# One 128-column product per 128 edges, with edge rows copied beside gathered rows, in a graph-attention kernel

## The chip, the cores and the metric

The kernel runs on one core of a Trainium2 chip. The metric is the device time of one execution in microseconds, the median of several runs. The core's engines are named as in the profile: PE (matrix products, with PEld for its weight loads), DVE (vector), ACT (scalar activation), POOL (here it issues the indirect gathers) and SP (here it issues plain transfers).

## The reference

A graph of 12500 nodes has 400000 edges, sorted by destination; every node and every edge has 64 features. One attention layer is computed, followed by a layer norm:

```
h_src = x[src];  h_dst = x[dst]
e     = leaky_relu(concat(h_src, h_dst, edge) @ W_attn + b_attn, 0.01)
m     = concat(h_src, edge) @ W_ne
alpha = softmax of e over the edges of one destination
z     = segment_sum(alpha * m, dst)
out   = relu(concat(x, z) @ W_out)
y     = layernorm(x + out)
```

## The kernel before

**Tiling.** Because sums over edges are linear, the kernel sums the weighted raw rows (edge row and gathered source row, 64 features each) per destination and applies `W_ne` once at the end. The sorted edges are cut into 782 groups of 512 (128 partitions, T = 4 edges on each). SG = 4 groups are a *part*, the unit of loads, scores and sums. Up to BG = 32 groups are a *batch*, the unit of the softmax; the list `sizes` holds 30, then 23 batches of 32, then 12 and 4.

**One batch** (the loop at the end of `sorted_path`) does the following.

- `gather` (L134) loads a part's edge rows into `ze` by one transfer of 512 KB on SP's queue, and issues one indirect gather on POOL for every 128 edges (L149), 16 for a part, into `zx`. The gathered row holds the 64 features of the source node and, from the second batch on, its share of the score as a 65th value. In the first batch the rows come from `x` itself, and the share is computed on DVE (L169 and L171).
- `scores` (L155) makes the score of each edge: DVE multiplies and reduces `ze` (L165, L167), adds the source's share (L172), builds the one-hot tile `hot` of each edge's slot among 48 consecutive destinations (L174), and picks the destination's share with it (L179, L182) out of `win`, which PE broadcasts from a row `wrow` (L161). L184 leaves the scores in `y`.
- `softmax` (L224) turns a batch's scores around (L252, then `e` on ACT, L254), runs scans on DVE with small products on PE between them, carries maximum and sum over to the next batch, and leaves `alpha` in PSUM (L309).
- `aggregate` (L321) makes `w` = `hot` times `alpha` on DVE (L324), multiplies on PE (L332), and adds the result to the running sums `acc` at the group's first destination on DVE (L342). Each float32 product is two PE instructions. For 128 edges there are two products, one of the edge rows, which goes to partitions 0 to 63 of `pg`, and one of the gathered rows, which goes to partitions 64 to 127. That is 64 PE instructions for a part.

**What sets the order.** A scheduler lays the operations out on the engines by their dependences and by the buffers of the pools; each engine then works in the order laid out. The pool `feats` holds ZB = 11 buffers each of `ze` and `zx`, so a gather waits until the `aggregate` eleven parts earlier has read its buffer. `hot` has HB = 9 buffers, `w` and `pg` have two each, `win` and `alpha` one each. A small PSUM tile `fixed` holds the slot numbers and two rows of attention weights. `indices` (L99) makes the gathers' indices `srcs` two batches ahead out of `raw` (transfer), `nat` (ACT, L112) and transposes on PE (L115). `neighbours` (L203) loads the destinations `d3` that the softmax's scans use, and fills the tile first when a batch has fewer than 32 groups.

**Start and end.** Before the batches, a prologue writes `table` (features and source shares) and `sdflat` (destination shares), spreads the latter with a transfer to `shifted`, and gathers from it 7 times on POOL (`wk`, L422) into `wins`, from which the rows `wrow` are read. Five parts' gathers are issued ahead of those 7 in the source (the list `ahead`). In the third batch and the ones after it, `own_part` (L432) is called after a part's `aggregate`, 25 times in all: it makes the product of `x` with its half of `W_out` and stores it in `early`. After the last batch, `finish_sorted` (L491) applies the weights to `acc` (L538), adds `early`, and makes the layer norm.

Of the kernel before, what the change touches and what calls it, by code (L numbers as in the profile page):

```python
# [9 lines left out]
F32 = mybir.dt.float32  # L10
I32 = mybir.dt.int32
AF = mybir.ActivationFunctionType
OP = mybir.AluOpType
AX = mybir.AxisListType

P = 128
T = 4
# [8 lines left out]
S = 48  # L26
BG = 32
SG = 4
HQ = 4
EW = 65  # L30
ZB = 11
HB = 9
NBC = 4

BF16 = mybir.dt.bfloat16
# [3 lines left out]
def sorted_path(ctx, tc, x, dst, idx, edge, w_ne, w_attn, b_attn, w_out, out, flag):  # L39
# [6 lines left out]
    nc = tc.nc  # L46
    N, D = x.shape
    E = edge.shape[0]
    NB = (N + P - 1) // P
# [33 lines left out]
    shifted = dram.tile([NB * P, S], F32, name="shifted")  # L83
# [7 lines left out]
    feats = loop.enter_context(tc.tile_pool(name="feats", bufs=ZB))  # L91
    psum = loop.enter_context(tc.tile_pool(name="psum", bufs=2, space=bass.MemoryType.PSUM))

    fixed = psum.tile([P, S + 2 * D], F32, name="fixed", bufs=1)
    slots = fixed[:, 0:S]
    w_edge = fixed[:, S:S + D].unsqueeze(1)
    w_src = fixed[:, S + D:S + 2 * D].unsqueeze(1)

    def indices(g0, G):  # L99

# [32 lines left out]

    def gather(g0, n, srcs, b0, plain):  # L134

        ze = feats.tile([P, SG, T, D], F32, name="ze")
        zx = feats.tile([P, SG, T, EW], F32, name="zx")
        whole = min(n, NG - 1 - g0)
        if whole:
            nc.sync.dma_start(out=ze[:, 0:whole].rearrange("p g t f -> p g (t f)"),  # L140
                              in_=edge[g0 * GE:(g0 + whole) * GE, :].rearrange("(g p t) f -> p g (t f)", g=whole, t=T))
        if whole < n:
            nc.vector.memset(ze[:, n - 1], 0.0)
            nc.sync.dma_start(out=ze[0:RP, n - 1],
                              in_=edge[E - REST:E, :].rearrange("(p t) f -> p t f", t=T))
        for g in range(n):
            for t in range(T):
                at = srcs[:, t, g0 + g - b0:g0 + g - b0 + 1]
                nc.gpsimd.indirect_dma_start(  # L149
                    out=zx[:, g, t, 0:D] if plain else zx[:, g, t, :], out_offset=None,  # L150
                    in_=x[:, :] if plain else table[:, :],
                    in_offset=bass.IndirectOffsetOnAxis(ap=at, axis=0))
        return ze, zx

    def scores(g0, n, ze, zx, drel, b0, y, plain):  # L155

        b = g0 - b0
        wrow = tiny.tile([1, SG, S], F32, name="wrow")
        nc.sync.dma_start(out=wrow[:, 0:n, :], in_=wins[g0:g0 + n, :].unsqueeze(0))
        win = psum.tile([P, SG, S], F32, name="win", bufs=1)  # L160
        nc.tensor.matmul(win[:, 0:n, :], ones_row, wrow[:, 0:n, :], start=True, stop=True)  # L161

        yb = y[:, :, b:b + n].rearrange("p t g -> p g t")
        prod = work.tile([P, SG, T, D], F32, name="prod", bufs=1)
        nc.vector.tensor_tensor(prod[:, 0:n], ze[:, 0:n],  # L165
                                w_edge.unsqueeze(1).to_broadcast([P, n, T, D]), op=OP.mult)
        nc.vector.tensor_reduce(yb, prod[:, 0:n], axis=AX.X, op=OP.add)  # L167
        if plain:
            nc.vector.tensor_tensor(prod[:, 0:n], zx[:, 0:n, :, 0:D],  # L169
                                    w_src.unsqueeze(1).to_broadcast([P, n, T, D]), op=OP.mult)  # L170
            nc.vector.tensor_reduce(zx[:, 0:n, :, D], prod[:, 0:n], axis=AX.X, op=OP.add)  # L171
        nc.vector.tensor_tensor(yb, yb, zx[:, 0:n, :, D], op=OP.add)  # L172
        hot = work.tile([P, SG, T, S], BF16, name="hot", bufs=HB)
        nc.vector.tensor_tensor(  # L174
            hot[:, 0:n], slots.unsqueeze(1).unsqueeze(1).to_broadcast([P, n, T, S]),
            drel[:, :, b:b + n].rearrange("p t g -> p g t").unsqueeze(3).to_broadcast([P, n, T, S]),
            op=OP.is_equal)
        at = work.tile([P, SG, T, D], F32, name="prod", bufs=1)[:, :, :, 0:S]
        nc.vector.tensor_tensor(at[:, 0:n], hot[:, 0:n],  # L179
                                win[:, 0:n].unsqueeze(2).to_broadcast([P, n, T, S]), op=OP.mult)  # L180
        sdst = tiny.tile([P, SG, T], F32, name="sdst")
        nc.vector.tensor_reduce(sdst[:, 0:n], at[:, 0:n], axis=AX.X, op=OP.add)  # L182
        nc.vector.tensor_tensor(sdst[:, 0:n], sdst[:, 0:n], yb, op=OP.add)
        nc.vector.scalar_tensor_tensor(yb, sdst[:, 0:n], SLOPE, sdst[:, 0:n], op0=OP.mult, op1=OP.max)  # L184
        return hot
# [38 lines left out]
    def softmax(G, y, d3, carry, first):  # L224


        R = HQ * G
# [77 lines left out]
                                sm.rearrange("r (q t) -> r q t", t=T), op=OP.mult)  # L305
        alpha0 = rows.tile([P, T, BG], F32, name="alpha0")
        nc.vector.transpose(alpha0.rearrange("p t g -> p (t g)"), al.rearrange("r t q -> r (t q)"))
        alpha = psum.tile([P, T, BG], F32, name="alpha", bufs=1)
        nc.scalar.activation(alpha, alpha0, AF.Copy)  # L309
        fac = None  # L310
        if not first:
# [4 lines left out]
            nc.tensor.matmul(pfac[:, 0:1], ones_row, fac1, start=True, stop=True)  # L316
            fac = tiny.tile([P, 1], F32, name="fac")
            nc.vector.tensor_copy(fac, pfac[:, 0:1])
        return alpha, fac, (top[:, R:R + 1], den[:, R:R + 1])

    def aggregate(g0, n, ze, zx, hot, alpha, b0, fac):  # L321
        b = g0 - b0
        w = work.tile([P, SG, T, S], F32, name="w")
        nc.vector.tensor_tensor(  # L324
            w[:, 0:n], hot[:, 0:n],
            alpha[:, :, b:b + n].rearrange("p t g -> p g t").unsqueeze(3).to_broadcast([P, n, T, S]),
            op=OP.mult)
        pg = psum.tile([P, SG, P], F32, name="pg")[:, :, 0:S]
        for g in range(n):
            for t in range(T):  # L330
                for at, z in ((0, ze), (D, zx)):
                    nc.tensor.matmul(pg[at:at + D, g, :], z[:, g, t, 0:D], w[:, g, t, :],  # L332
                                     start=(t == 0), stop=(t == T - 1))
        _, vs = nc.values_load_multi_w_load_instructions(
            d0i[0:1, g0:g0 + n], engines=(EngineType.DVE,), min_val=0, max_val=N - 1,
            skip_runtime_bounds_check_because=within)
        for g in range(n):
            if g == 0 and fac is not None:
                a1 = acc[:, ds(vs[0], 1)]
                nc.vector.tensor_scalar(a1, a1, fac, None, op0=OP.mult)  # L340
            ag = acc[:, ds(vs[g], S)]
            nc.vector.tensor_tensor(ag, ag, pg[:, g, :], op=OP.add)  # L342


    sizes = []
    left = NG
    for short in (SG, 3 * SG):
        sizes.insert(0, short)
        left -= short
    while left > 0:  # L350
        sizes.insert(0, min(left, BG))
        left -= sizes[0]
    starts = [sum(sizes[:k]) for k in range(len(sizes))]

# [22 lines left out]
    with tc.tile_pool(name="pre", bufs=2) as pre:  # L377
# [34 lines left out]
        zero = pre.tile([1, S], F32, name="zero", bufs=1)  # L412
        nc.vector.memset(zero, 0.0)
        nc.scalar.dma_start(out=sdflat[NB * P:NB * P + S].unsqueeze(0), in_=zero)
        while len(ahead) < 5 and (len(ahead) + 1) * SG <= sizes[0]:
            ahead.append(gather(len(ahead) * SG, SG, prepared[0][0], 0, True))
        over = sdflat[0:1]
        nc.sync.dma_start(out=shifted, in_=bass.AP(over.tensor, over.offset, [[1, NB * P], [1, S]]))
        for k in range(NW):
            m = min(P, NG - k * P)  # L420
            wk = pre.tile([P, S], F32, name="wk")
# [10 lines left out]
    def own_part(c0):  # L432
# [8 lines left out]
            nc.scalar.dma_start(out=xb[:, 0:nf, :],  # L441
                                in_=x[c0 * P:(c0 + nf) * P, :].rearrange("(b p) f -> p b f", p=P))
        xtt = work.tile([D, NBC, P], F32, name="xtt", bufs=1)
        pxt = psum.tile([P, NBC, P], F32, name="pg")
        for j in range(n):
            nc.tensor.transpose(pxt[0:D, j, :], xb[:, j, :], ident)
        nc.scalar.activation(xtt[:, 0:n, :], pxt[0:D, 0:n, :], AF.Copy)  # L447
        po = psum.tile([P, NBC, P], F32, name="pg")[:, :, 0:D]
        for j in range(n):
            nc.tensor.matmul(po[:, j, :], xtt[:, j, :], wout[:, 0, :], start=True, stop=True)  # L450
        xo = work.tile([P, NBC, D], F32, name="xo", bufs=1)
# [8 lines left out]
    with loop:  # L460
        carry = None
        own = 0
        ready = {k: prepare(k) for k in range(2)}
        for k, G in enumerate(sizes):
            b0 = starts[k]
            srcs, drel = ready.pop(k)
            d3 = neighbours(b0, G)
            y = rows.tile([P, T, BG], F32, name="y", bufs=2)
            if G < BG:
                nc.vector.memset(y[:, :, G:BG], 0.0)  # L470
            parts = []
            for g0 in range(b0, b0 + G, SG):
                n = min(SG, b0 + G - g0)
                ze, zx = ahead.pop(0) if ahead else gather(g0, n, srcs, b0, k == 0)
                hot = scores(g0, n, ze, zx, drel, b0, y, k == 0)
                parts.append((g0, n, ze, zx, hot))
            if k + 2 < len(sizes):
                ready[k + 2] = prepare(k + 2)
            alpha, fac, carry = softmax(G, y, d3, carry, k == 0)
            for g0, n, ze, zx, hot in parts:  # L480
                aggregate(g0, n, ze, zx, hot, alpha, b0, fac if g0 == b0 else None)
                if own < NB and k > 1:
                    own_part(own)
                    own += NBC
        while own < NB:
            own_part(own)
            own += NBC
# [518 lines left out]
```

## Time and profile before

| | us |
|---|---|
| median of 3 runs (lowest, highest) | 4106.01 (4105.14, 4106.99) |
| the profiled execution | 5109.14 |
| its span | 5107.4 |
| POOL busy in it | 2964.9 |
| DVE busy | 1708.1 |
| PE busy | 1410.6 |
| ACT busy | 109.6 |

The profiled execution is longer than the timed runs. Its mean granted PE clock is 0.547 of full speed. A row of the costliest groups reads: line, engine, operation, output and inputs with their shapes, number of instructions, then busy time and mean nanoseconds of one, then the idle time just before these instructions and what ended most of it. In a timeline a line gives the start, the duration, the instruction, and in brackets the idle time before it with its releaser; "issue" is time in which the engine waited for nothing that the profile shows.

### The profile page before, as it was taken

What the parts mean: (1) busy time and instruction counts of PE and PEld (TensorE: products, weight loads), DVE (VectorE), ACT (ScalarE), POOL (GpSimd) and SP (SyncE); (2) the same over time, 40 slices, a digit from 0 to 9 for tenths busy, and PEclk for the clock granted to TensorE, in tenths of its full rate; (3) what the DMA queues carried; (4) which work ended last, traced back from release to release, by engine and by line L of the source; (5) the groups of instructions that cost most, each with busy time, mean ns of one, the idle gap of its engine ahead of it and who ended that gap; (6) DMA issues with size and microseconds to landing.
All of it is one profiled execution on the core that took longest, in us unless ns stands there. A gap on an engine that the chain in (4) does not pass through costs nothing.

```text
span 5107.4 us, 39846 instructions
## 1 busy us (share of the span) xinstructions
PE 1410.6 (28%) x14238; PEld 1105.0 (22%) x14238; DVE 1708.1 (33%) x4006; ACT 109.6 (2%) x239; POOL 2964.9 (58%) x3142
## 2 busy tenths in 40 slices
PE   0022233443222222222222222222222222222226
PEld 0012122332222122212121212122222211221225
DVE  3333233232342332332323323323233233233346
ACT  0000000000000000000000000000000000000001
POOL 6645656556556556565565565655655655656550
PEclk9975555555555555555555555555555555555555
DMA  6111122222111112111111111111111211212113
GB/s 145 25 34 42 44 48 54 53 53 60 41 45 44 43 38 48 42 46 41 43 44 43 42 44 43 43 42 44 47 41 40 47 42 38 47 37 48 41 36 77
DMA packets 315273, 239.73 MB, mean 47 GB/s; under 512 B 160576, under 2 KB 264235, under 8 KB 315064
## 3 DMA queue, kind: packets, MB, share of 16 engines
q0 software_dynamic: 100320, 104.41, 10.6%
q1 hardware_dynamic: 147464, 116.22, 8.0%
q10 hardware_dynamic: 67280, 16.45, 1.6%
q8 instruction: 115, 1.88, 0.2%
q14 instruction: 94, 0.77, 0.1%
HBM read 226.98 MB, written 12.28 MB: 47 GB/s over the span
## 4 chain that ended last, share of the span: by engine, by line
issue 28%; POOL 26%; another core or an unknown queue 19%; DVE 14%; PE 10%; DMA 3%; DVEq 1%; ACT 0%; POOLq 0%; ACTq 0%
POOL zx L149 26%; PE pg L332 7%; DMA zx<-table,srcs 2%; DVE y L167 2%; DVE prod L165 2%; DVE sdst L182 1%; DVE prod L179 1%; PE sm L198 1%; PE sm L190 1%; DVE hot L174 1%; DVE w L324 1%; DVE by_row L195 0%; DVE b L271 0%; DVE acc L342 0%
## 5 line engine op out<-in xcount | busy, mean ns | idle before, releaser
L149 POOL DMA_INDIRECT zx<-table,srcs x3008 | 2840.6, 944 | 1951.4 <-issue 841.3
L332 PE MATMUL pg<-w,ze 128*64 128x48 f32 x6256 | 792.3, 297 | 1640.2 <-issue 985.1
L332 PEld LDWEIGHTS pg<-w,ze 128*64 128x64 f32 x6256 | 703.6, 213 | 1729.3 <-issue 1581.7
L332 PE MATMUL pg<-w,zx 128*64 128x48 f32 x6256 | 803.4, 297 | 613.2 <-issue 582.1
L324 DVE TENSOR_TENSOR w<-hot,alpha 128x768 f32<-128x768 bf16 x196 | 184.0, 949 | 2208.2 <-remote 1135.9
L332 PEld LDWEIGHTS pg<-w,zx 128*64 128x64 f32 x6256 | 706.7, 213 | 656.3 <-issue 621.7
L342 DVE TENSOR_TENSOR acc<-acc,pg 128x48 f32 x782 | 153.9, 197 | 812.7 <-remote 742.1
L161 PE MATMUL win<-wrow,ones_row 1*128 1x192 f32 (+1 forms) x392 | 182.0, 552 | 746.8 <-DVE prod L179 433.1
L161 PEld LDWEIGHTS win<-wrow,ones_row 1*128 1x128 f32 x392 | 92.9, 284 | 810.4 <-DVE prod L179 448.3
L165 DVE TENSOR_TENSOR prod<-ze,fixed 128x1024 f32<-128x1024 f32 x196 | 236.9, 1209 | 19.9 <-issue 19.9
L167 DVE TENSOR_REDUCE y<-prod 128x16 f32<-128x1024 f32 x196 | 236.1, 1205 | 2.4 <-DVE y L184 2.3
L182 DVE TENSOR_REDUCE sdst<-prod 128x16 f32<-128x768 f32 x196 | 185.1, 944 | 4.3 <-DVE prod L179 2.4
L179 DVE TENSOR_TENSOR prod<-hot,win 128x768 f32<-128x768 bf16 x196 | 185.4, 946 | 0.9 <-issue 0.2
L174 DVE TENSOR_TENSOR hot<-fixed,drel 128x768 bf16<-128x768 f32 x196 | 185.6, 947 | 0.0
L149 POOL DMA_INDIRECT zx<-in_x_dram,srcs x120 | 116.9, 974 | 51.5 <-issue 36.3
L112 ACT ACTIVATE nat<-raw 32x1024 f32<-32x1024 int32 (+3 forms) x26 | 27.5, 1056 | 3242.2 <-PE pp L115 1762.9
L450 PE MATMUL pg<-wout,xtt 64*128 64x64 f32 x196 | 47.4, 418 | 132.0 <-ACT xtt L447 132.0
L198 PE MATMUL sm<-ones_row,by_row 1*128 1x1 f32 x208 | 59.2, 351 | 81.2 <-DVE by_row L195 66.2
L198 PEld LDWEIGHTS sm<-ones_row,by_row 1*128 1x128 f32 x208 | 50.9, 302 | 131.5 <-DVE by_row L195 104.2
L190 PE MATMUL sm<-order,b 128*1 128x128 f32 x104 | 30.1, 391 | 163.8 <-DVE b L271 158.4
L450 PEld LDWEIGHTS pg<-wout,xtt 64*128 64x128 f32 x196 | 42.8, 319 | 148.3 <-ACT xtt L447 148.3
L190 PE MATMUL sm<-order,s 128*1 128x128 f32 x104 | 30.3, 393 | 147.7 <-issue 57.1
(133 smaller groups left out, 949.1 us busy)
## 6 DMA issues: line engine op xcount, KB each, us to landing
ze<-in_edge_dram SPq DMA_DIRECT2D x194, 512.0 KB
zx<-table,srcs POOLq DMA_INDIRECT x3008
table<-xt ACTq DMA_DIRECT2D x14, 227.5 KB
wrow<-wins SPq DMA_DIRECT2D x195, 0.8 KB
xb<-in_x_dram ACTq DMA_DIRECT2D x24, 128.0 KB
early<-xo ACTq DMA_DIRECT2D x24, 128.0 KB
xb<-in_x_dram ACTq DMA_DIRECT2D x12, 256.0 KB
xo<-early SPq DMA_DIRECT2D x12, 256.0 KB
```

The lines of the kernel that those rows point to most:

```text
L149: nc.gpsimd.indirect_dma_start(out=zx[:, g, t, 0:D] if plain else zx[:, g, t, :], out_offset=None, in_=x[:, :] if plain else table[:, :], ...
L161: nc.tensor.matmul(win[:, 0:n, :], ones_row, wrow[:, 0:n, :], start=True, stop=True)
L165: nc.vector.tensor_tensor(prod[:, 0:n], ze[:, 0:n], w_edge.unsqueeze(1).to_broadcast([P, n, T, D]), op=OP.mult)
L167: nc.vector.tensor_reduce(yb, prod[:, 0:n], axis=AX.X, op=OP.add)
L174: nc.vector.tensor_tensor(hot[:, 0:n], slots.unsqueeze(1).unsqueeze(1).to_broadcast([P, n, T, S]), drel[:, :, b:b + n].rearrange("p t g -> ...
L179: nc.vector.tensor_tensor(at[:, 0:n], hot[:, 0:n], win[:, 0:n].unsqueeze(2).to_broadcast([P, n, T, S]), op=OP.mult)
L182: nc.vector.tensor_reduce(sdst[:, 0:n], at[:, 0:n], axis=AX.X, op=OP.add)
L190: nc.tensor.matmul(p[0:1, :], col, order, start=True, stop=True)
L198: nc.tensor.matmul(p[:, 0:1], by_row, ones_row[:, 0:1], start=True, stop=True)
L324: nc.vector.tensor_tensor(w[:, 0:n], hot[:, 0:n], alpha[:, :, b:b + n].rearrange("p t g -> p g t").unsqueeze(3).to_broadcast([P, n, T, S]) ...
L332: nc.tensor.matmul(pg[at:at + D, g, :], z[:, g, t, 0:D], w[:, g, t, :], start=(t == 0), stop=(t == T - 1))
L342: nc.vector.tensor_tensor(ag, ag, pg[:, g, :], op=OP.add)
```

## The change

The two tiles `ze` and `zx` of `feats` become one tile `z`, with 129 values for each edge: a copy of the edge row, the gathered row, and the source's share. `ze` is still loaded by SP, now into a pool with three buffers; ACT copies it into `z` in `scores`. One product of 128 columns then takes the place of the two of 64. `win` and `alpha` move into `fixed`, which becomes 512 values wide. `w` and `pg` get four buffers instead of two, `z` has 9 (`ze` and `zx` had 11), `hot` 8 instead of 9. Batches have 24 groups (32 of them), and the last two have 10 and 4. Three parts instead of five are gathered ahead of the 7 gathers of the prologue, and the transfer that writes `shifted` is issued on ACT's queue instead of SP's. Lines of the changed kernel lie 1 to 4 lower: its product is L334, its sum L346, its `e` L258, its copy L166.

```diff
+BS = 24
-ZB = 11
-HB = 9
+ZW = 129
+ZB = 9
+HB = 8
...
-    fixed = psum.tile([P, S + 2 * D], F32, name="fixed", bufs=1)
+    fixed = psum.tile([P, 512], F32, name="fixed", bufs=1)
...
+    alpha = fixed[:, S + 2 * D:S + 2 * D + T * BG].rearrange("p (t g) -> p t g", t=T)
+    win = fixed[:, S + 2 * D + T * BG:S + 2 * D + T * BG + SG * S].rearrange("p (g s) -> p g s", g=SG)
...
-        ze = feats.tile([P, SG, T, D], F32, name="ze")
-        zx = feats.tile([P, SG, T, EW], F32, name="zx")
+        z = feats.tile([P, SG, T, ZW], F32, name="z")
+        ze = chunks.tile([P, SG, T, D], F32, name="ze", bufs=3)
...
-                    out=zx[:, g, t, 0:D] if plain else zx[:, g, t, :], out_offset=None,
+                    out=z[:, g, t, D:2 * D] if plain else z[:, g, t, D:ZW], out_offset=None,
...
-        win = psum.tile([P, SG, S], F32, name="win", bufs=1)
         nc.tensor.matmul(win[:, 0:n, :], ones_row, wrow[:, 0:n, :], start=True, stop=True)

+        nc.scalar.activation(z[:, 0:n, :, 0:D], ze[:, 0:n], AF.Copy)
...
-        alpha = psum.tile([P, T, BG], F32, name="alpha", bufs=1)
         nc.scalar.activation(alpha, alpha0, AF.Copy)
...
-        w = work.tile([P, SG, T, S], F32, name="w")
+        w = work.tile([P, SG, T, S], F32, name="w", bufs=4)
...
-        pg = psum.tile([P, SG, P], F32, name="pg")[:, :, 0:S]
+        pg = psum.tile([P, SG, P], F32, name="pg", bufs=4)[:, :, 0:S]
         for g in range(n):
             for t in range(T):
-                for at, z in ((0, ze), (D, zx)):
-                    nc.tensor.matmul(pg[at:at + D, g, :], z[:, g, t, 0:D], w[:, g, t, :],
-                                     start=(t == 0), stop=(t == T - 1))
+                nc.tensor.matmul(pg[:, g, :], z[:, g, t, 0:2 * D], w[:, g, t, :],
+                                 start=(t == 0), stop=(t == T - 1))
...
-    for short in (SG, 3 * SG):
+    for short in (SG, 10):
...
-        sizes.insert(0, min(left, BG))
+        sizes.insert(0, min(left, BS))
...
-        while len(ahead) < 5 and (len(ahead) + 1) * SG <= sizes[0]:
+        while len(ahead) < 3 and (len(ahead) + 1) * SG <= sizes[0]:
...
-        nc.sync.dma_start(out=shifted, in_=bass.AP(over.tensor, over.offset, [[1, NB * P], [1, S]]))
+        nc.scalar.dma_start(out=shifted, in_=bass.AP(over.tensor, over.offset, [[1, NB * P], [1, S]]))
```

More of the change, by code (lines that the diff above doesn't have):

```diff
@@ L149, in gather, with scores @@
                 nc.gpsimd.indirect_dma_start(
-                    out=zx[:, g, t, 0:D] if plain else zx[:, g, t, :], out_offset=None,
+                    out=z[:, g, t, D:2 * D] if plain else z[:, g, t, D:ZW], out_offset=None,
                     in_=x[:, :] if plain else table[:, :],
                     in_offset=bass.IndirectOffsetOnAxis(ap=at, axis=0))
-        return ze, zx
-    def scores(g0, n, ze, zx, drel, b0, y, plain):
+        return ze, z
+    def scores(g0, n, ze, z, drel, b0, y, plain):
         b = g0 - b0
@@ L168, in scores @@
         if plain:
-            nc.vector.tensor_tensor(prod[:, 0:n], zx[:, 0:n, :, 0:D],
+            nc.vector.tensor_tensor(prod[:, 0:n], z[:, 0:n, :, D:2 * D],
                                     w_src.unsqueeze(1).to_broadcast([P, n, T, D]), op=OP.mult)
-            nc.vector.tensor_reduce(zx[:, 0:n, :, D], prod[:, 0:n], axis=AX.X, op=OP.add)
-        nc.vector.tensor_tensor(yb, yb, zx[:, 0:n, :, D], op=OP.add)
+            nc.vector.tensor_reduce(z[:, 0:n, :, 2 * D], prod[:, 0:n], axis=AX.X, op=OP.add)
+        nc.vector.tensor_tensor(yb, yb, z[:, 0:n, :, 2 * D], op=OP.add)
         hot = work.tile([P, SG, T, S], BF16, name="hot", bufs=HB)
@@ L318, in softmax, with aggregate @@
             nc.vector.tensor_copy(fac, pfac[:, 0:1])
-        return alpha, fac, (top[:, R:R + 1], den[:, R:R + 1])
-    def aggregate(g0, n, ze, zx, hot, alpha, b0, fac):
+        return fac, (top[:, R:R + 1], den[:, R:R + 1])
+    def aggregate(g0, n, z, hot, b0, fac):
         b = g0 - b0
-        w = work.tile([P, SG, T, S], F32, name="w")
+        w = work.tile([P, SG, T, S], F32, name="w", bufs=4)
         nc.vector.tensor_tensor(
@@ L443, in own_part @@
         xtt = work.tile([D, NBC, P], F32, name="xtt", bufs=1)
-        pxt = psum.tile([P, NBC, P], F32, name="pg")
+        pxt = psum.tile([P, NBC, P], F32, name="pg", bufs=4)
         for j in range(n):
@@ L447, in own_part @@
         nc.scalar.activation(xtt[:, 0:n, :], pxt[0:D, 0:n, :], AF.Copy)
-        po = psum.tile([P, NBC, P], F32, name="pg")[:, :, 0:D]
+        po = psum.tile([P, NBC, P], F32, name="pg", bufs=4)[:, :, 0:D]
         for j in range(n):
@@ L473, in sorted_path @@
                 n = min(SG, b0 + G - g0)
-                ze, zx = ahead.pop(0) if ahead else gather(g0, n, srcs, b0, k == 0)
-                hot = scores(g0, n, ze, zx, drel, b0, y, k == 0)
-                parts.append((g0, n, ze, zx, hot))
+                ze, z = ahead.pop(0) if ahead else gather(g0, n, srcs, b0, k == 0)
+                hot = scores(g0, n, ze, z, drel, b0, y, k == 0)
+                parts.append((g0, n, z, hot))
             if k + 2 < len(sizes):
                 ready[k + 2] = prepare(k + 2)
-            alpha, fac, carry = softmax(G, y, d3, carry, k == 0)
-            for g0, n, ze, zx, hot in parts:
-                aggregate(g0, n, ze, zx, hot, alpha, b0, fac if g0 == b0 else None)
+            fac, carry = softmax(G, y, d3, carry, k == 0)
+            for g0, n, z, hot in parts:
+                aggregate(g0, n, z, hot, b0, fac if g0 == b0 else None)
                 if own < NB and k > 1:
```

## The prediction

> **What bounds the kernel now.** I read the page first, then the waits of POOL, then single stretches of the timeline.
>
> ```profile
> PE 1410.6 (28%) x14238; PEld 1105.0 (22%) x14238; DVE 1708.1 (33%) x4006; ACT 109.6 (2%) x239; POOL 2964.9 (58%) x3142
> ...
> L149 POOL DMA_INDIRECT zx<-table,srcs x3008 | 2840.6, 944 | 1951.4 <-issue 841.3
> L332 PE MATMUL pg<-w,ze 128*64 128x48 f32 x6256 | 792.3, 297 | 1640.2 <-issue 985.1
> ...
> L112 ACT ACTIVATE nat<-raw 32x1024 f32<-32x1024 int32 (+3 forms) x26 | 27.5, 1056 | 3242.2 <-PE pp L115 1762.9
> ```
>
> POOL issues one gather per 128 edges and is the busiest engine. What keeps it idle stands in its waits (total, times, longest):
>
> ```profile
> POOL zx L149 <- issue: 877.5, 2825, 8.4
> POOL zx L149 <- PE pg L332: 786.6, 62, 61.1
> POOL zx L149 <- remote: 252.8, 80, 3.8
> ```
>
> POOL's timeline, at the first stall and at one in the middle, says how they look: a gather takes 0.94 us, the next starts 0.30 later, so the pace is 1.2475 us, until the rows' buffer is not free.
>
> ```profile
> 299.67 0.94 POOL L149 DMA_INDIRECT zx<-table,srcs  x1 [61.13 <-PE pg L332]
> ```
> ```profile
> 2702.90 0.94 POOL L149 DMA_INDIRECT zx<-table,srcs  x1 [0.30 <-issue]
> 2724.84 0.95 POOL L149 DMA_INDIRECT zx<-table,srcs  x1 [20.99 <-PE pg L332]
> ```
>
> Why is the releaser late? In PE's timeline a part's 64 instructions run as pairs 0.107 us apart (32 pairs, 3.4 us), and then, in mid part, PE falls to steps of 2.1 us with nothing that it waits for:
>
> ```profile
> 2547.51 0.24 PE L332 MATMUL pg<-w,zx 128*64 128x48 f32 x1 [2.56 <-issue]
> 2549.61 0.24 PE L332 MATMUL pg<-w,zx 128*64 128x48 f32 x1 [1.86 <-issue]
> ```
>
> The profiled execution took 5109.14 us (span 5107.4, so 1.7 around it), the timed runs 4106.01: 1003.1 less. POOL's waits on PE and "remote" sum to 1039.4 (786.6 + 252.8), nearly the same. So I sum the timed run as if the slow PE steps belonged to the profiled execution alone. First gather at 16.7; 3128 gathers and 7 of L422 at 1.2475 make 3911; the prologue's stall 61.1, of which some 16 is a stretch of DVE in the same slow steps (223 to 262 us), so 45; then the tail. In the profile the tail is 136.8 (last gather ends 4970.6). Without slow PE, the 12-group batch's scores end some 12 us before the last gather instead of 13 after it; alpha follows 24.7 later, the last alpha 22 later, its aggregate 5.7, `finish_sorted` 70.7: 111. Sum 16.7 + 3911 + 45 + 111 + 1.7 = 4085; 21 us are left over for small stalls. **The timed kernel is bound by the number of gathers**, and the change keeps that number.
>
> [...]
>
> **The change, part by part.**
>
> *One product instead of two (L332).* 12512 PE instructions become 6256. At full pace nothing is gained: the halves run side by side now, 32 x 0.107 = 3.4 us a part. The nearest row for the merged one is L538, 128 columns, 64 moving: 80 in 17.33 us, 0.217 each. With 48 moving I take 0.15 to 0.21: 4.8 to 6.7 us a part, 1.4 to 3.3 us more. Only the first of a batch is on the way to POOL's next buffer.
>
> *The copy (ACT, new).* 196 x 1.06 us (row `nat`, as many elements per partition) = 207 us on an engine busy for 109.6; about 6.4 a batch of six. It hides under 120 us of gathers per batch. It could wait on a late edge transfer and stand ahead of the softmax's own ACT steps (the copies of the next batch's first three parts and `nat` do stand ahead of `e` in ACT's order). Edge buffers fall from 11 to 3: the sixth part's is free once DVE has read the third before it, about 13 us before the last gather, so the copy is done some 8 us before. Cost 0 to 5 us.
>
> *Batches of 24, ZB 9.* Eight more softmaxes (about 22 us each) and their transfers, all under gathers. Reach: 9 buffers less 6 parts is 3 parts, as 11 less 8 was, 3 x 16 x 1.2475 = 59.9 us from a batch's last gather to the first gather that needs a released buffer. After that last gather: landing and last scores 7, softmax 22, first w, product 7: 36. So 24 us remain, before and after; no steady stall to remove, and none made.
>
> *Four buffers of w and pg; win and alpha inside `fixed`.* DVE's order changes by it: six w, sums, and only then the next batch's scores; before, these were interleaved. In mid run that delays scores by 6 x 5 = 30 us, which have 120 us of gathers to catch up. Zero there, up to 21 gained if the 21 us left over are waits on those buffers. Memory shared with `slots`: no new order of instructions follows; 0.
>
> *Start.* POOL stops when its buffers are full: now after 10.5 parts (batch 0 has 30 groups, so its last part is a half) and 7 gathers of L422, at 238.5 us, 3 more than 16.7 + 175 x 1.2475; then after nine parts, 144 + 7 gathers, so about 208. The first release is at 299.7, or 284 without slow DVE. It comes earlier by one and a half parts of scores of 7.93 us (11.9) and by 2.5, as the last gather of L422, which the first scores wait for, moves from 187.6 to about 185; later by 2 for the product and up to 3 for the copies ahead of `e`: 272 to 275. The stall is 64 to 67 instead of 45: **+19 to +22**. `shifted`'s DMA goes from SP's queue, where it stands beside edge loads, to ACT's; who waits for it are the gathers of L422 on POOL, counted in the 2.5. Three parts instead of five gathered ahead of them change no count.
>
> *Tail.* Sizes end 24, 10, 4 instead of 32, 12, 4. Let X be the last gather's end. The last 24-batch's alpha is at X - 41 (its last gather at X - 70). Then six parts of PE, 29 to 40 us, then, behind most of their sums in DVE's order, the 10-batch's scores, 2.5 x 5.35 = 13: they end at X - 2 to X + 8, against X - 12. Alpha +25; three w and ten groups' products 11 to 14; behind eight of the sums the last part's scores, 6; its softmax 22, aggregate 5, finish 71: X + 136 to X + 150 against X + 111. Before, the last part's scores were done between the sums of the batch before. If PE is quicker than 0.15 the interleaving wins back up to 10: **+15 to +39**, I take 24.
>
> Sum: 20 + 24 + 2 for the copies in mid run, less 6, as I count on a part of the leftover going: +40, so **4146 us**. In the profiled execution the sign may differ: half the PE records should leave fewer slow steps; I expect its span at 4400 to 4950, with POOL's wait on PE under 600.
>
> **The rivals.**
>
> *PE's slow steps are in the timed runs too* (faster). Then the gather's 0.30 us gap must be the profiler's: 3135 x 0.944 = 2959, and with 1039 of stalls 16.7 + 2959 + 1039 + 137 = 4152, some 1% above the time, so the gap would have to go wholly and something more besides. The sum above misses by 0.5% with nothing adjusted but the tail and start. If so, half as many PE instructions take away a quarter to half of the stalls, 260 to 520 us: 3590 to 3850, less if DVE's scores come next.
>
> *The leftover is waits on w and pg* (faster or same). It decides where start and tail cost under 20 together: 4080 to 4098 where they cost nothing, 4098 to 4114 where they cancel. For it: every product waits for a sum two parts back. Against it: 24 us of reach.
>
> *ACT's order makes the softmax late* (slower). Place: `e`, L254, behind copies that wait for edge transfers. It decides once a batch is late by more than the 24 us of reach; at 40 late, 16 x 33 batches = 530 us, 4640. A transfer takes 2.5 us and SP is nearly idle, so I give it little.
>
> **How the numbers follow.** 0.2%, 8 us, is about what a measurement of this kernel tells from no change. Gather-bound with dearer ends, 4120 to 4185: 0.59. Ends and leftover cancelling: 0.10. Leftover removed: 0.11. Slow PE real: 0.16. ACT late: 0.04. So faster 0.27, same 0.10, slower 0.63. The range must leave out no more than 0.2: the last two cases; it runs from 4075 to 4185. The likeliest case's own is 4120 to 4185.
>
> **What would show it.** In the changed profile: 6256 products of 128*128; POOL at 1.25 us a gather; a first stall from about 208 to 275; `nat`-like copies of 1.1 us; scores of the 10-batch ending after the last gather; 165 us or less from last gather to end. Wrong if the time falls under 4075 while POOL's pace stays, or if POOL's gathers in the middle of the run wait for ACT or DVE in every batch.

## The result, and the profile after

The changed kernel takes 4143.66 us (median of four runs, 4143.47 to 4145.79) beside 4106.2: a ratio of 1.0093, 95% interval 1.0075 to 1.011, or 37.5 us more. The forecast was 4146. The profiled execution is one of the four runs, 4143.47 with a span of 4141.7. The experiments below ran on five chips, on which the kernel before takes 5108.7 to 5133.0 us in its timed runs too, about as long as the profile with the PE steps shown in the prediction (5109.14); so each of them is read by its ratio to the kernel before on the same chip, and none shows directly what its edit does where PE has no steps. Whether one of the five gave the result is not known.

The page of the changed kernel, the busy line and the rows that answer to those of before:

```profile
PE 1914.2 (46%) x8238; PEld 1683.6 (41%) x8238; DVE 1860.2 (45%) x4448; ACT 333.3 (8%) x483; POOL 2966.5 (72%) x3142
...
L153 POOL DMA_INDIRECT z<-table,srcs x3032 | 2865.2, 945 | 982.7 <-issue 929.4
L334 PE MATMUL pg<-w,z 128*128 128x48 f32 x6256 | 1348.0, 413 | 75.3 <-DVE w L327 72.6
...
L166 ACT ACTIVATE z<-ze 128x1024 f32<-128x1024 f32 x196 | 207.6, 1060 | 2787.3 <-DMA z<-table,srcs 2557.9
```

POOL is as busy in microseconds as before, and its share has risen to 72%. PE's idle time on "issue" in the products, 985.1 us for one of the two halves before, is gone; that is not the change's doing, for a run of the same kernel below has it again. The sums of the changed kernel stand at L344. ACT's copies take 1060 ns each, beside 1056 for `nat` before.

POOL's waits, and its timeline at the only stall that is left:

```profile
POOL z L153 <- issue: 958.1, 2951, 59.0
POOL z L153 <- DMA z<-table,srcs: 33.2, 109, 0.3
POOL z L153 <- DVE srcs L122: 14.1, 1, 14.1
POOL z L153 <- PE pg L334: 10.1, 33, 0.3
```
```profile
206.10 0.94 POOL L153 DMA_INDIRECT z<-table,srcs  x1 [0.30 <-issue]
266.10 0.94 POOL L153 DMA_INDIRECT z<-table,srcs  x1 [59.05 <-issue]
...
3994.12 0.94 POOL L153 DMA_INDIRECT z<-table,srcs  x1 [0.30 <-issue]
```

After that stall every gather follows the last by 0.3 us to the end. The whole span is a sum of four terms: the first gather at 15.5, 3134 times a mean pace of 1.2507 (3919.7; the pace is what the other three terms leave), 58.75 for the stall beyond the usual gap, and 147.6 from the start of the last gather (3994.12) to the end. In the middle of the run the products of a batch are one burst of 192 instructions, and all six window products of the next batch (the broadcasts of `win`, L164) stand behind it. PE's timeline there, with the first of the six:

```profile
2518.92 41.20 PE L334 MATMUL pg<-w,z 128*128 128x48 f32 x192 [2.08 <-DVE w L327]
2560.05 1.00 PE L164 MATMUL fixed<-wrow,ones_row 1*128 1x192 f32 x2
```

And the tail, first on DVE, then on PE:

```profile
3989.35 1.22 DVE L169 TENSOR_TENSOR prod<-ze,fixed 128x1024 f32<-128x1024 f32 x1 [7.08 <-PE fixed L164]
...
4004.14 0.31 DVE L256 STREAM_TRANSPOSE er<-y 128x128 f32<-128x128 f32 x1
...
4020.53 2.28 DVE L327 TENSOR_TENSOR w<-hot,fixed 128x768 f32<-128x768 bf16 x3 [0.41 <-ACT fixed L312]
...
4039.81 1.22 DVE L169 TENSOR_TENSOR prod<-ze,fixed 128x1024 f32<-128x1024 f32 x1 [3.42 <-PE fixed L164]
```
```profile
4021.53 17.30 PE L334 MATMUL pg<-w,z 128*128 128x48 f32 x80 [2.09 <-DVE w L327]
...
4063.42 7.06 PE L334 MATMUL pg<-w,z 128*128 128x48 f32 x32 [3.76 <-DVE w L327]
```

The last gather ends at 3995.06. The 10-batch's scores begin late because the window product waits behind the burst, and its softmax starts 9 us after that gather; not all of the wait of 7.1 us is lost, since that gather's own rows are needed too. The last part's scores then wait 3.4 us for their window product behind the 80 products, as the 10-batch's did.

### The profile page after: what moved, and what is told of

It is laid out like the page before. It is cut to its first block, busy times and chain, and to the rows that moved or that the text cites. A ratio compares the mean times of both kernels' runs of the same rounds, so it can differ in the third digit from the quotient of the medians.

```text
span 4141.7 us, 29721 instructions
## 1 busy us (share of the span) xinstructions
PE 1914.2 (46%) x8238; PEld 1683.6 (41%) x8238; DVE 1860.2 (45%) x4448; ACT 333.3 (8%) x483; POOL 2966.5 (72%) x3142
## 3 DMA queue, kind: packets, MB, share of 16 engines
q0 software_dynamic: 100320, 104.42, 15.5%
## 4 chain that ended last, share of the span: by engine, by line
POOL 43%; PE 22%; issue 17%; DVE 10%; DMA 7%; ACT 1%; ACTq 0%; POOLq 0%; DVEq 0%; SPq 0%
POOL z L153 42%; PE pg L334 17%; DMA z<-table,srcs 6%; PE sm L202 2%; PE sm L194 2%; DVE by_row L199 1%; DVE b L275 1%; DVE w L327 1%; PE pg L452 1%; DVE prod L169 0%; DVE col L204 0%; ACT z L166 0%; DVE y L171 0%; PE fixed L164 0%; DVE prod L183 0%
## 5 line engine op out<-in xcount | busy, mean ns | idle before, releaser
L153 POOL DMA_INDIRECT z<-table,srcs x3032 | 2865.2, 945 | 982.7 <-issue 929.4
L334 PE MATMUL pg<-w,z 128*128 128x48 f32 x6256 | 1348.0, 413 | 75.3 <-DVE w L327 72.6
L334 PEld LDWEIGHTS pg<-w,z 128*128 128x128 f32 x6256 | 1338.8, 333 | 95.3 <-DVE w L327 89.2
L164 PE MATMUL fixed<-wrow,ones_row 1*128 1x192 f32 x392 | 196.3, 602 | 1543.8 <-DVE prod L183 1458.9
L164 PEld LDWEIGHTS fixed<-wrow,ones_row 1*128 1x128 f32 x392 | 97.2, 306 | 1625.3 <-DVE prod L183 1535.3
L344 DVE TENSOR_TENSOR acc<-acc,pg 128x48 f32 x782 | 157.8, 202 | 685.9 <-PE pg L334 674.3
L166 ACT ACTIVATE z<-ze 128x1024 f32<-128x1024 f32 x196 | 207.6, 1060 | 2787.3 <-DMA z<-table,srcs 2557.9
L327 DVE TENSOR_TENSOR w<-hot,fixed 128x768 f32<-128x768 bf16 x196 | 179.0, 943 | 153.8 <-PE pg L334 152.1
L183 DVE TENSOR_TENSOR prod<-hot,fixed 128x768 f32<-128x768 bf16 x196 | 185.6, 947 | 0.1
L153 POOL DMA_INDIRECT z<-in_x_dram,srcs x96 | 93.9, 978 | 43.0 <-issue 28.6
L119 PE MATMUL pp<-ident,nat 24*128 24x24 f32 (+2 forms) x272 | 36.3, 279 | 143.2 <-DVE drel L128 103.8
```

The costliest lines, as they stand in the source:

```text
L153: nc.gpsimd.indirect_dma_start(out=z[:, g, t, D:2 * D] if plain else z[:, g, t, D:ZW], out_offset=None, in_=x[:, :] if plain else table[:, :],
L166: nc.scalar.activation(z[:, 0:n, :, 0:D], ze[:, 0:n], AF.Copy)
L183: nc.vector.tensor_tensor(at[:, 0:n], hot[:, 0:n], win[:, 0:n].unsqueeze(2).to_broadcast([P, n, T, S]), op=OP.mult)
L327: nc.vector.tensor_tensor(w[:, 0:n], hot[:, 0:n], alpha[:, :, b:b + n].rearrange("p t g -> p g t").unsqueeze(3).to_broadcast([P, n, T, S]) ...
L334: nc.tensor.matmul(pg[:, g, :], z[:, g, t, 0:2 * D], w[:, g, t, :], start=(t == 0), stop=(t == T - 1))
```

## The experiments

A ratio below is to the kernel before on the same chip, with its 95% interval.

**Batches of 24 alone.**
```diff
+BS = 24
...
-ZB = 11
+ZB = 9
...
-    for short in (SG, 3 * SG):
+    for short in (SG, 10):
...
-        sizes.insert(0, min(left, BG))
+        sizes.insert(0, min(left, BS))
```


> The kernel before with batches of 24 groups, last batches of 10 and 4, and 9 row buffers; two products per 128 edges, the scheduling of sums and the prologue as before. If the start costs by the batches (nine parts gathered at the first stall instead of ten and a half, first release 12 us earlier) and the tail by the product and the order of the sums: +17 us from the start and about 0 from the tail, 4123 us. If the whole loss belongs to the merged product and its order: 4106. If all of it to the batches: 4144.

Measured: 5186.37, 1.0116 (1.0101 to 1.013). Its first stall is 67.1 us against 61.1, its tail from the start of the last gather 126.2 against 137.8 (spans 5180.0 and 5107.4, last gathers 5053.81 and 4969.63). So the batches and their nine buffers cost something, but here neither in the tail nor, beyond 6 us, in the first stall: the last gather is 84 us later, and most of that lies between the two. None of the absolute times expected could be tested with the steps there.

**Two products in the changed kernel.**
```diff
-                nc.tensor.matmul(pg[:, g, :], z[:, g, t, 0:2 * D], w[:, g, t, :],
-                                 start=(t == 0), stop=(t == T - 1))
+                for at in (0, D):
+                    nc.tensor.matmul(pg[at:at + D, g, :], z[:, g, t, at:at + D], w[:, g, t, :],
+                                     start=(t == 0), stop=(t == T - 1))
```


> The changed kernel with the two products of 64 columns side by side in place of the one of 128, read from the same tile z. If the merged product is dearer at full pace (7.06 us a part in the changed kernel's profile against 3.4): the first release comes 3.6 earlier, the ten groups' products before the last scores take 9 less, the last part's 3.6 less: 4128 us. If the product count matters (64 PE instructions a part make the sums late): slower than 4144, by up to 200 us. If product width costs nothing: 4144.

Measured: 5665.28, 1.1045 (1.1031 to 1.106). The changed kernel itself comes to 1.0852 on another chip (below): the merged product is 1.8% to the good where PE has steps, and far more than the products separates this kernel from the one before.

**Two buffers of `w` and `pg` in the changed kernel.**
```diff
-name="w", bufs=4)
+name="w", bufs=2)
...
-name="pg", bufs=4)
+name="pg", bufs=2)
```


> The changed kernel with two buffers of w and pg instead of four, so that DVE's order again has the last part's scores among the sums of the batch before. If that order costs the tail 6 us of scores and 3 us of waiting for the last window product: 4134 to 4138 us. If four buffers carry something in the middle of the run (sums that gathers wait for): above 4150. If the order is worth nothing: 4144.

Measured: 5690.31, 1.1096 (1.107 to 1.1121). In PE's order one window product comes back among the products, the other five stay behind them. So it is not mainly the four buffers that make that order, as the prediction had it.

**Half the products in the kernel before.**
```diff
-                for at, z in ((0, ze), (D, zx)):
+                for at, z in ((D, zx),):
...
-            ag = acc[:, ds(vs[g], S)]
-            nc.vector.tensor_tensor(ag, ag, pg[:, g, :], op=OP.add)
+            ag = acc[D:P, ds(vs[g], S)]
+            nc.vector.tensor_tensor(ag, ag, pg[D:P, g, :], op=OP.add)
```


> The kernel before without the products of the edge rows: 32 PE instructions a part instead of 64, the sums made for the gathered rows' 64 features alone (the edge rows' part of the aggregate is left out). Gathers are as many as before. If the timed kernel is bound by the number of gathers: 4094 to 4106 us. If the slow PE steps of the profiled execution are in the timed runs as well: 260 to 520 us less, 3590 to 3850. Its profile, with fewer PE records, should show the start and the tail of the kernel before less disturbed.

Measured: 5153.02, 1.0045 (1.0031 to 1.006). Half the PE instructions bring nothing even where PE has steps. That tells against the rival in which fewer PE instructions gain 260 to 520 us; the steps are, by the times, in timed runs, but the time did not follow the number of instructions. PE's idle time on "issue" fell in the products from 1567.2 us (985.1 and 582.1 for the two halves) to 610.4, but at the window products it is now 1499.0, where all idle time before was 746.8.

```profile
2562.12 6.70 PE L332 MATMUL pg<-w,zx 128*64 128x48 f32 x64 [2.41 <-DVE w L324]
```

This run also shows what a half costs alone: 64 instructions of 64 columns take 6.70 us, 0.105 each, so a pair at a pace of 0.107 is two of them side by side, not one after the other. The changed kernel's merged product takes 0.213 to 0.214 us from start to start in mid burst: twice a pair.

**One gather more per part in the kernel before.**
```diff
+                if g == 0 and t == 0:
+                    nc.gpsimd.indirect_dma_start(...)   # the same gather again
```


> The kernel before with one more gather per part: the part's first gather is issued twice into the same place, 196 gathers more. If gathers bound the time, 196 x 1.25 = 245 us more than the kernel before beside it. If POOL is held by late sums instead (the steps of PE that nothing explains), its stalls of 21, 7, 7, 3, 3 and 3 us a batch swallow part of the 10 us more per batch: about 60 to 150 us more.

Measured: 5391.88 beside 5108.7, 1.0547 (1.0528 to 1.0566): 283 us, 1.44 for each gather added, which is more than the pace of 1.25. The stalls did not swallow it; beyond the usual gap they are 1079 us in its profile against 1035 in the profile of before. The gathers are on the path in full, stalls or not.

**The changed kernel again.** No edit.

> The changed kernel unaltered, beside the same runs of the kernel before as the other kernel of this job. Where the kernel before takes 4106: 4143 again. Where it takes some 5130, with PE in steps of 0.7 us an instruction after a burst: if the merged product, with half the PE instructions, suffers less from these steps: under 5130; if the batch's six parts of products in one burst run into them more: 5500 to 5700, as the two variants of the changed kernel did beside 5128.

Measured: 5540.47, 1.0852 (1.0821 to 1.0883), the second of the two cases: a loss of 8.5%, where the run without steps showed 0.9%. PE's timeline of this run shows where the burst breaks, and POOL's shows what happens at the break's end:

```profile
2455.42 24.13 PE L334 MATMUL pg<-w,z 128*128 128x48 f32 x112 [2.08 <-DVE w L327]
2480.17 0.45 PE L334 MATMUL pg<-w,z 128*128 128x48 f32 x2 [0.62 <-issue]
...
2527.21 0.24 PE L334 MATMUL pg<-w,z 128*128 128x48 f32 x1 [2.56 <-issue]
...
2530.74 8.10 PE L334 MATMUL pg<-w,z 128*128 128x48 f32 x37 [0.49 <-issue]
```
```profile
2531.51 0.94 POOL L153 DMA_INDIRECT z<-table,srcs  x1 [4.36 <-issue]
```

After 112 product instructions at 0.215 us, PE takes 50 us for the next 43, and returns to full speed at 2530.74. POOL had stopped at 2527.15 (2531.51 less 4.36). This is no single case. Count as a phase eight or more steps of over 0.5 us from start to start, with at most six quicker ones in a row between them, after which PE returns to its pace, and as a stop a pause of POOL of over 2 us: all 28 phases of the run end 3.5 to 7.7 us after POOL has stopped.

Two causes that lie near are ruled out by this run beside the one of the result. Both are profiles of the same kernel (29721 instructions in that of the result), so recording does not by itself make the steps. And both give PE's granted clock as 1.000, so a lower clock is not what sets them apart.

**`win` and `alpha` in tiles of their own**, in the changed kernel; `pg` and `w` have two buffers.
```diff
+        win = psum.tile([P, SG, S], F32, name="win", bufs=1)
...
+        alpha = psum.tile([P, T, BG], F32, name="alpha", bufs=1)
```


> The changed kernel with win and alpha in PSUM tiles of their own again (and so two buffers of pg and w[...]): one product of 128 columns, copies, batches of 24 as in the changed kernel. Of its order one sees before the run that the window products and the next batch's scores stand between the products again, where the changed kernel has all six parts' products in one burst and five of six window products behind it. If the shared tile is what puts the scores behind the burst, and this is what costs: beside a kernel before of 4106, 4125 to 4135 (the start's cost stays); beside one of 5110 to 5130, a ratio of 1.00 to 1.03 instead of 1.085 to 1.11. If the cost is in the product's width, the copy or the three edge buffers: 4144, and a ratio of 1.07 to 1.11.

Measured: 5243.6, 1.0222 (1.0208 to 1.0236). Against 1.1096 with both in `fixed` and as many buffers, most of the loss is the shared tile.

**`alpha` alone in a tile of its own, two buffers.**

> The changed kernel with alpha alone in a tile of its own and two buffers of pg and w: against the run with win and alpha apart (ratio 1.022) only win is put back into fixed; against the run with both in fixed and two buffers (1.110) only alpha is taken out. If alpha in the tile that the scores read is the cause: 1.015 to 1.03. If win in that tile costs as well: 1.05 to 1.11. If three and four buffers, and not win, made the last run's 1.055: again 1.015 to 1.03. Beside a kernel before of 4106: 4120 to 4135.

Measured: 5244.11, 1.0247 (1.0226 to 1.0267). It is `alpha`: with `win` back in `fixed` the ratio hardly moves. Every score reads `fixed` (the slots and the edge weights), and once `alpha` is written into that tile, the order laid out puts the next batch's scores behind the softmax and its products. That the scheduler does so because it orders by whole tiles is argued from the two orders. Without `alpha` there the window products stand in between, as PE's timeline of this run shows:

```profile
2347.82 13.89 PE L334 MATMUL pg<-w,z 128*128 128x48 f32 x64 [2.08 <-DVE w L327]
2363.74 1.00 PE L163 MATMUL fixed<-wrow,ones_row 1*128 1x192 f32 x2 [2.02 <-DVE prod L182]
2364.67 7.06 PE L334 MATMUL pg<-w,z 128*128 128x48 f32 x32
```

**`alpha` apart, three buffers of `pg` and four of `w`.**

> The changed kernel with alpha alone in a PSUM tile of its own; win stays in fixed, pg gets three buffers, w four. Before the run one sees the next batch's window products and scores stand among the products again. If it is alpha in the tile that all scores read that orders them behind the softmax: a ratio of 1.00 to 1.025 where PE has steps (1.022 with both tiles apart and two buffers); 4120 to 4135 beside 4106 where it has none. If win in the tile does it: 1.08 and more, or 4143.

Measured: 5401.6, 1.0549 (1.0508 to 1.059), between the two cases. With the run above, which differs in the buffers alone, the 3% are the buffers': in mid run 128 product instructions stand in a row in PE's order, where two buffers had 64. With `alpha` shared more buffers had gained (1.0852 against 1.1096). Why their sign turns stays open, and so does how much `alpha` alone costs with the changed kernel's four buffers.

**First batch cut into 14 and 16 groups, kernel before.**
```diff
+    sizes[0:1] = [14, sizes[0] - 14]
```


> The kernel before with its first batch of 30 groups cut into 14 and 16. If POOL's first stall is the wait for the first batch's scores and softmax, four parts of scores at 7.93 us less come before the first release, the stall shrinks from 61 to about 29 us, and the time falls by 32 us: 4074 beside 4106, or 5077 to 5097 beside 5110 to 5130. If another batch only moves the stall to the next release: no change within 8 us.

Measured: 5130.64 beside 5133.01, 1.0000 (0.9992 to 1.0009). A miss for the first case. POOL's timeline, its stalls of the start:

```profile
102.40 0.95 POOL L149 DMA_INDIRECT zx<-table,srcs  x1 [14.35 <-DMA sdflat<-sdt]
121.84 0.94 POOL L423 DMA_INDIRECT wk<-shifted,d0p  x1 [7.24 <-DMA shifted<-sdflat]
286.50 0.95 POOL L149 DMA_INDIRECT zx<-table,srcs  x1 [28.64 <-PE pg L332]
```

The stall for buffers did fall to 28.6 us. But with fewer gathers from `x` to issue, POOL reached the gathers that need the prologue's tables before those were written, and waited 14.4 and 7.2 us there; the remaining 11 did not show in the time.

**The kernel before again.** No edit.

> The kernel before unaltered, for one profile. Where PE has no steps of 0.7 us: 4106, first stall 45 us, 112 from the start of the last gather to the end, and 11 us of small stalls. Where it has them: 5110 to 5130 with a first stall of 61, as in the profile shown before.

Measured: 5114.27, first stall 61.05: a profile with steps again. The first case was not met on any of the chips.

**Seven buffers of `z` in the changed kernel.**
```diff
-ZB = 9
+ZB = 7
```


> The changed kernel with seven buffers of z instead of nine, so that POOL comes one part ahead of a batch instead of three and stops 40 us earlier in each. Where PE has no steps: some 16 to 20 us of stall in each of 33 batches, 4143 + 33 x 18 = about 4740. Where PE has steps: if it falls into them while gathers flow, and comes out once POOL stops, the stall of some 48 us a batch shrinks to 20 to 30 although POOL has fewer buffers: 4700 to 5100, against the changed kernel's 5540. If the steps have nothing to do with gathers: slower than 5540, by 10 to 30 us a batch, 5870 to 6500.

Measured: 5612.53, 1.0986 (1.0944 to 1.1029), outside all three cases. In the middle of the run a batch's long stall fell from some 34 to 29 us; but the first stall of all is 77.4 us instead of 61.1, and after 3500 us the long stalls are mostly 42 to 49 instead of 30 to 35. Of 43 phases of steps 41 end 3.6 to 7.8 us after POOL stops, the two others 8.9 after. In the middle they are shorter, two of some 29 and 38 us to a batch where one of 51 had been: as the stop came earlier, so did their end. The time itself decides nothing about what causes the steps.

## Why the prediction was right, and where it was not

**The bound.** Right. The changed kernel is gathers from 15.5 us to 3995.06 with one stall; the pace was put at 1.2475 and is 1.2507, 10 us over the run. That a gather keeps POOL as long when PE has half the product instructions was assumed; it takes 945 ns, beside 944 before. The 24 us of reach per batch held: none of the 33 later batches stalls POOL. An extra gather costs its full price, and somewhat more (1.44 us), even with stalls about.

**The start.** The stall begins where forecast (207 against "about 208") and ends at 266.1 instead of 272 to 275, so it is 59 us instead of 64 to 67. Two terms explain 4.5 us of it. The softmax was too large: from the scores' turn (240.78) to the first `w` (257.28) it takes 16.5 us where no step disturbs it, against 19.5 in the disturbed profile. And the last of the seven gathers moved by 4.0 us, not 2.5: it starts at 191.41 in the profile before, where the prediction has 187.6, and at 187.38 now. The rest was not taken apart.

```profile
240.78 0.31 DVE L256 STREAM_TRANSPOSE er<-y 128x128 f32<-128x128 f32 x1
...
257.28 3.55 DVE L327 TENSOR_TENSOR w<-hot,fixed 128x768 f32<-128x768 bf16 x4
```

**The tail.** Forecast 136 to 150 us after the last gather (its own terms add up to 138 to 151), of which 135 went into the sum; measured 146.6. Inside it the terms are off in both directions. The two softmaxes were put at 25 and 22 and take 16.4 (4004.14 to 4020.53) and 16.6. The scores of the 10-batch end 9 us after the last gather, beyond the forecast's 8. The product takes 0.215 to 0.221 us, not 0.15 to 0.21, so that ten groups take 17.3; the row L538 that the prediction read, 0.217 with 64 moving columns, was right as it stood, and lowering it for 48 was the mistake. From the first `w` of the ten groups to the last part's scores it is 19.3 us (4020.53 to 4039.81) against 11 to 14. The two waits for window products, 7.1 and 3.4 us, were not in the sum.

**The split between start and tail is not shown.** By the same sum the kernel before has 4104.3 - 16.7 - 3919.7 = 167.9 us for its stalls and its tail, the changed kernel 58.75 + 147.6 = 206.3; the 38.4 between them are the loss. The tail of before was put at 111 after the last gather's end, with the same long softmaxes. An estimate with 16.5 for each, from the changed kernel's profile, makes it 97, or 98 from the last gather's start; that its softmaxes, laid out among the sums of another batch, would be as short is not shown. Then 70 us are left for all stalls in the kernel before, and the tail has lost some 49 while stalls have won some 11. How the 70 divide is open: if the first stall was 42 (the forecast's 45 less 3 for the softmax), 28 were small stalls, all gone since, and the start lost 17. In the profiles with steps the tail is dearer too, and the start is not. First stalls: 61.1 before, 61.1 changed. From the start of the last gather to the end: 137.8 before, 172.4 changed (5535.4 - 5363.03), and 152.3 with `alpha` apart (5242.4 - 5090.15). A profile of the kernel before without steps would settle it; none was obtained.

**Luck.** In the forecast's terms the sum was 16.7 + 3911 + 65 + 135 + 1.7, and 17 for copies and the kept part of the leftover; measured are 15.5, 3921, 58.75, 146.6, 1.8 and 0. The 10 us of pace were 10 of the 21 left over, so they cancel. What remains is a tail 12 us too cheap against a start 6 us too dear and 7 us of small stalls and copies that are not there. That the sum came within 3 us is luck in part.

**Two steps of the reasoning failed.**

*"As if the slow PE steps belonged to the profiled execution alone."* They belong to some executions, timed ones among them. Where the kernel before takes 4106 the reading of the sum held. That recording brings the steps was the author's estimate, and no run shows it: on one chip of the experiments the kernel before takes 5114.27 us where it is profiled and 5099.12 to 5130.6 in its timed runs, halving the products' PE instructions left the time as it was (a ratio of 1.0045), and the profile of the result has no steps and is the fastest of its four runs. The forecast for the profiled execution, a span of 4400 to 4950 because half the PE records should leave fewer steps, was wrong both ways: 4141.7 in the run of the result, 5535.4 where the steps appear. What the runs show in its place is that the steps come in long phases (129 of the 133 counted in three profiles end within 9 us after a stop of POOL), and that those of the changed kernel are longer, mostly some 51 us against 17 to 29 in the profile of before.

*"Memory shared with `slots`: no new order of instructions follows; 0."* It does follow. The prediction saw the new order and gave it to the four buffers. The runs with two buffers give it to `alpha` in `fixed`: 1.0247 with `alpha` apart, 1.1096 with it inside. Without steps that order costs nothing in mid run, as the prediction said, because 120 us of gathers cover it: POOL never waits there. That it is paid in the tail, where nothing covers it, is argued from the two waits for window products; no run without steps has `alpha` apart.

**The rivals.** That fewer PE instructions make it faster falls with the half products. ACT's order did no harm: `e` is not held anywhere by a copy for longer than the reach, since POOL does not stall. That the leftover is waits on `w` and `pg` is not decided: the changed kernel has no small stalls, and how many the other had without steps is not known. The cause of the 37.5 us is thus argued from one profile, and not shown by an experiment.

No kernel tried beats the one before; the nearest, with the first batch cut, equals it on a chip with steps.

## What to carry to other kernels

Before sharing a tile, list who reads the rest of it: one late write into it can order all of those readers behind it (here 1.1096 with `alpha` in `fixed`, 1.0247 with it apart, where PE has steps). Such an order may cost nothing under a long stage and be paid at the end of the kernel, where there is no such stage; here that is argued, not shown. Where the profiled execution and the timed runs differ by a quarter, ask which of them the next chip will look like, and price the change for both. A sum can be right with two of its terms wrong, so read the stages of the new profile one by one.

## What the runs showed of the hardware that was not expected

In the profile of before and in those of the experiments PE falls, after a burst, into steps of 0.7 us and its multiples with nothing that the profile shows it waiting for (112 products at full speed, then 43 in 50 us; in that run most steps are of 0.7, 1.4, 2.1 or 2.8 us), and comes out 3.5 to 8.9 us after POOL stops issuing gathers, in all 71 phases counted in two runs (the changed kernel with nine and with seven buffers). In the run of the result the same burst of 192 product instructions runs through in 41.2 us with gathers beside it. In the profile of before 58 of 62 phases end 2.8 to 5.4 us after a stop; in the four others the products ran out. What holds PE in the steps is not shown.

A float32 product of 128 columns takes 0.213 to 0.214 us per PE instruction in mid burst, whether 48 or 64 columns move (192 in 41.20 us, 80 of L540 in 17.33), and one of 64 columns takes 0.105 to 0.107, alone or side by side with another. So one product in place of two side by side gains nothing at full pace.
